# The z product of half B from bf16 parts, and the x products dealt out over the steps anew, in a gated recurrence on one core

## The chip, the cores and the metric

The kernel runs on 1 core of a Trainium2 chip. The metric is the device time of one execution in microseconds (us). Before the change it is 1654.64 us, the median of 3 runs (1654.48 to 1655.43).

## The reference

A gated recurrent layer over T = 512 time steps with batch 8, 512 inputs and 512 state units, and a residual sum at the end:

```python
def step(h, x_t):
    fused = sigmoid(concatenate([x_t, h], -1) @ w_W + w_b)
    hidden_state, output_state = split(fused, 2, -1)         # r and z
    memory_state = x_t @ wx_W + wx_b + hidden_state * (h @ wh_W + wh_b)
    h_new = output_state * h + (1.0 - output_state) * tanh(memory_state)
    return h_new, h_new
out = x + scan(step, h0, x)          # all float32; x is (8, 512, 512)
```

Below, r and z are the two gates, "h" in a bank's content is `h @ wh_W`, and x products are `x_t` times its three weight matrices, which do not depend on the state.

## The kernel before

**Layout.** State units lie on partitions. The 512 units are four chunks k = 0 to 3 of 128 inputs; half A of the state is chunks 0 and 1, half B chunks 2 and 3. Each step's matmul has a state chunk as the stationary operand (128 x 32: four steps of 8 batch columns, three of them zero) and weights as the moving one. For each k there are four products j, one on each 32-column tile of TensorE, so the outputs stand on partitions 32j to 32j+31. An f32 matmul appears in the profile as two MATMULs with a LDWEIGHTS each.

**A step on TensorE** (loop over i, from line 565; order by `ORDER`, line 26): "A0 B0 A1 A2 A3 B1 B2 B3 C0 C1 C2 C3", a bank's letter and the state chunk k. Bank A (192 columns) holds h, z and r of half A, bank B (128) r and h of half B, and C (64) z of half B. C lies in the PSUM tile `cs` (64 columns for each parity of the group of four steps). In the profile `hTA` and `hTB` are the two halves of the state, `wa` and `wb` the weights, `wb` those of B and C.

Behind C come the x products of a later pair of groups (`x_step`, line 528). A group is four steps (GS), and one x product serves a group, so that two groups are worked on over eight steps; u is the step's place in these eight and o their number. `SLOTS` names seven slots of 384 columns of products of block sums (seven products instead of eight), and `SHARE` (line 48) gives the columns for each u. The products accumulate in `xps` and `eps`; ScalarE and VectorE combine them (lines 697 to 742) into the SBUF tiles `even` and `odd`, one for each group of the pair.

**x into the banks.** `spread` (line 448) copies the group's x part from `even` or `odd` to a bank on ScalarE, once in four steps; the C copy is at u = 1, 3 (last pair) and 7. `turn_x` transposes the part that goes into the memory state (`md1`).

**A step on VectorE and ScalarE.** VectorE transposes 128x64 pieces of the banks (`turn_r`, `turn_h`, `turn_z`; tiles `tr`, `md1`, `tz`), ScalarE applies the sigmoid to `tr` (into `md0`) and `tz` (into `hd0`, with scale -1). `memory(hf, q)` is a scan on VectorE that makes the memory state `m` of chunk q of a half, and a tanh on ScalarE into the state tile (`hTA<-m`, `hTB<-m`); `update(hf, q)` is the scan that writes the new state (`hTA<-hd0A,hTA`). The order on VectorE is that of lines 655 to 677: half A's transposes and scans; r and h of half B; update(0,0); z of half B; update(0,1), which also waits for r of half B's sigmoid; memory(1,0), memory(1,1), update(1,0), update(1,1). Behind it two ScalarE copies (`hTA<-hTA`, `hTB<-hTB`) put the new state into a second slot. GpSimd adds x to the new state for the output (`ot`, lines 750 to 771), and SyncE stores four steps at a time.

**Order.** All instructions are collected by `Flow`, and each engine works through its own in the order of the program. `plan` adds semaphore waits: a reader for the last writer, a writer for readers, and for PSUM any engine for the last access of every other engine in that tile and partition quarter.

**State tiles.** `hT` are eight tiles for each half; a tile holds 32 columns (four steps) in three slots.

Of the kernel before, what the change touches and what calls it, by code (L numbers as in the profile page):

```python
# [8 lines left out]
F32 = mybir.dt.float32  # L9
# [5 lines left out]
P = 128  # L15
NQ = 4
# [70 lines left out]
class Flow:  # L87
# [44 lines left out]
    def plan(self):  # L132
# [9 lines left out]
        for i, item in enumerate(self.items):  # L142
# [70 lines left out]
            snap[me] = order[i]  # L213
            done.append(snap)

    def emit(self, tc):

        self.plan()
        sems = {e: tc.alloc_semaphore(f"flow_{e}") for e in self.ENGINES}
        lanes = [tc.alloc_semaphore(f"flow_dma{n}") for n in range(self.LANES)]  # L220
        count = {}
        with tc.tile_critical():
            for item in self.items:
                engine = getattr(self.nc, item.engine)
                for other in sorted(item.waits, key=lambda o: o.index):
                    engine.wait_ge(other.sem, other.value)
                inst = getattr(self, item.op, getattr(engine, item.op, None))(*item.args, **item.kw)  # L227
# [11 lines left out]
def tile_cond_rnn_residual(  # L239
# [132 lines left out]
    for n, t_ in enumerate(hd0[0] + hd0[1] + md0[0] + md0[1] + hT[0] + hT[1]):  # L372
        (nc.vector if n < DVE_FILL else nc.gpsimd).memset(t_, 0.0)
    for t_ in hd0[0] + hd0[1]:
        nc.gpsimd.memset(t_[:, :, :, 1], -1.0)
    idle = const.tile([P, IDLE], F32, name="idle")
# [9 lines left out]
    def state(hf, i, slot=2):  # L386
# [5 lines left out]
    wide = [{n: psum.tile([P, 512], F32, name=f"{n}{q}") for n in "AB"} for q in range(2)]  # L392
    banks = [
        {"A": wide[q]["A"][:, : BANKS["A"]],
         "B": wide[q]["B"][:, : BANKS["B"]],
         "C": cs[:, HU * q : HU * q + HU]}
        for q in range(2)
    ]
    xps = [psum.tile([P, 512], F32, name=f"xp{q}") for q in range(2)]
    piece = psum.tile([P, 512], F32, name="eps")  # L400
    eps = piece[HI, :W]

    def mm(out_, lhsT, rhs, start=False):
        nc.tensor.matmul(
# [122 lines left out]

    def x_step(o, u):

        at = sum((SHARE * 2)[5 : u if u > 4 else u + 8]) - SHARE[5] // 3  # L530
        o += 2 if u > 4 else 1
        end = at + SHARE[u]
        while at < end:
            n, c0 = divmod(at, W)
            c1 = min(W, c0 + end - at)
            for pair_, (name, k) in enumerate(SLOTS[n % 7]):
                product(o + n // 7 - (n % 7 == 0 and pair_ == 0), name, k, c0, c1)
            at += c1 - c0
# [14 lines left out]
            for t_ in (even, odd):  # L553
                nc.gpsimd.tensor_copy(t_, bias)
    keep(0)
    spread(0, "ABC")
    for hf in range(2):
        turn_x(0, hf)
    keep(1)
# [5 lines left out]
    for i in range(T):  # L565
# [8 lines left out]
        for n in (ORDER if i else FIRST).split():  # L574
            if n == "x":
                take(first[3], 1)
                continue
            bank, k = n[0], int(n[1])
            hs = hT[k // 2][i % NH][:, :, k % 2, 2]
# [9 lines left out]
        def scan(c_, out_, d0, d1):  # L589
# [8 lines left out]
        pa = ps["A"]  # L598
        raw = {
            "h": (pa[:, :HU], ps["B"][:, HU:]),  # L600
            "z": (pa[:, HU : 2 * HU], ps["C"]),
            "r": (pa[:, 2 * HU :], ps["B"][:, :HU]),
        }

# [57 lines left out]
        turn_r(1)  # L662
        turn_h(1)
        update(0, 0)
        turn_z(1)
        nc.after(update(0, 1), r_done[1])
        if i == T - 1:
            nc.gpsimd.tensor_tensor(
                ot[:, t, :2, :].rearrange("p c n -> p n c"),
# [1 line left out]
                state(0, T),  # L671
                ALU.add,
            )
        memory(1, 0)
        memory(1, 1)
        update(1, 0)
        update(1, 1)
        for hf in range(2):
            act(state(hf, i + 1, 0), state(hf, i + 1), AF.Copy)
        if i < 3:  # L680
            inst = load_x(i + 1)
            if i == 0:
                nc.after(inst, r_done[1])
# [6 lines left out]
        if o == LAST:  # L690
            if u == 2:
                spread(2 * o + 1, "AB")
                turn_x(2 * o + 1, 0)
                turn_x(2 * o + 1, 1)
            elif u == 3:
                spread(2 * o + 1, "C")
        elif u == 0:
            if o == 0:
                spread(1, "A")
            if sums:  # L700
                nc.scalar.copy(reg(BE), reg(AL))
                nc.scalar.copy(both[LO], reg(DE))
                x_sum(o + 1, 3)
            turn_x(2 * o + 1, 0)
            turn_x(2 * o + 1, 1)
        elif u == 1:
            if sums:
                nc.scalar.copy(more[HI], eps)
            spread(2 * o + 1, "BC" if o == 0 else "AC")
        elif u == 2:  # L710
            if sums:
                nc.vector.tensor_tensor(reg(GA), reg(BE), more[HI], ALU.add)
                nc.scalar.copy(even[LO, XC], reg(AL))
            if o:
                spread(2 * o + 1, "B")
        elif u == 3:
            if sums:
                nc.vector.tensor_tensor(odd[HI, XC], reg(GA), both[LO], ALU.add)
                nc.scalar.copy(both[HI], reg(DE))
            if two:  # L720
                x_sum(o + 2, 2)
        elif u == 4:
            if o == 0:
                keep(3)
            if two:
                nc.scalar.copy(reg(AL), bias[LO, XC])
                x_sum(o + 2, 0)
        elif u == 5:
            if sums:
                nc.vector.tensor_tensor(even[HI, XC], reg(BE), both[HI], ALU.add)  # L730
            if two:
                nc.scalar.copy(reg(DE), step_bias[HI])
        elif u == 6 and nxt:
            spread(2 * o + 2, "AB")
            turn_x(2 * o + 2, 0)
        elif u == 7 and nxt:
            if o:
                nc.scalar.copy(odd[LO, XC], reg(GA))
            spread(2 * o + 2, "C")
            turn_x(2 * o + 2, 1)  # L740
            if two:
                x_sum(o + 2, 1)
# [107 lines left out]
```

## Time and profile before

| | |
|---|---|
| median of 3 runs | 1654.64 us (1654.48 to 1655.43) |
| profiled execution | 1657.46 us; span of its instructions 1655.7 us |
| TensorE granted clock, mean | 0.999 |
| TensorE matmul busy | 1645.6 us (99%) |
| VectorE, ScalarE, GpSimd busy | 1153.9 (70%), 1193.8 (72%), 301.9 (18%) us |
| instructions | 125580 |

A row of the groups view names line, engine, operation, output and inputs with their shape, the count, then busy us, mean ns of one, and idle time before with what ended it. All operations have line 227 because `Flow` issues them. A row of a timeline has start in us, duration, engine, operation, output and inputs and the count of neighbours taken together; in brackets stands the wait before it and what ended that.

### The profile page before, as it was taken

How to read it: one execution, taken by the hardware profiler on the slowest of the kernel's cores; microseconds unless marked ns; L12 is line 12 of the kernel's file. 1: busy time of each engine (PE TensorE's matmuls, PEld its weight loads, DVE VectorE, ACT ScalarE, POOL GpSimd, SP SyncE). 2: the span in 40 equal slices, each digit the busy share in tenths (PEclk: the TensorE clock that was granted, in tenths of full speed). 3: DMA queues.
4: the chain of work that ended last, by engine and by line, in shares of the span. 5: the costliest groups of instructions: out<-in, count | busy, mean ns of one | idle time of the engine just before them, and what ended most of it. 6: DMA issues, size and time to landing. Idle time of an engine off the chain costs nothing.

```text
span 1655.7 us, 125580 instructions
## 1 busy us (share of the span) xinstructions
PE 1645.6 (99%) x54298; PEld 1500.2 (91%) x54298; DVE 1153.9 (70%) x9194; ACT 1193.8 (72%) x5998; POOL 301.9 (18%) x1279
## 2 busy tenths in 40 slices
PE   9999999999999999999999999999999999999998
PEld 5999999999999999999999999999999999999987
DVE  6776676676766766767667767677676766766765
ACT  3777777777777777777777777777777777777775
POOL 1211111111111111111111111111111111111111
PEclk9999999999999999999999999999999999999999
DMA  4000000000000000000000000000000000000000
GB/s 182 11 18 14 15 15 16 16 14 15 16 15 15 14 16 16 14 14 15 16 15 14 14 17 14 15 14 17 14 14 15 17 14 14 15 17 10 10 10 10
DMA packets 37284, 31.14 MB, mean 19 GB/s; under 512 B 4084, under 2 KB 35060, under 8 KB 36600
## 3 DMA queue, kind: packets, MB, share of 16 engines
q1 hardware_dynamic: 36576, 22.89, 4.5%
q8 instruction: 424, 6.95, 1.7%
q14 instruction: 132, 1.08, 0.2%
q10 hardware_dynamic: 152, 0.22, 0.1%
HBM read 14.70 MB, written 8.39 MB: 14 GB/s over the span
## 4 chain that ended last, share of the span: by engine, by line
PE 99%; DVE 1%; issue 0%; ACT 0%; DVEq 0%; SPq 0%
PE A L227 40%; PE B L227 26%; PE xp L227 18%; PE cs L227 13%; PE eps L227 1%; DVE tr L227 0%; DVE m L227 0%; DVE tz L227 0%; DVE md1B L227 0%; DVE md1A L227 0%; DVE hTA L227 0%; DVE hTB L227 0%; ACT hTB L227 0%; DVE zeros L227 0%; DVE rows L227 0%
## 5 line engine op out<-in xcount | busy, mean ns | idle before, releaser
L227 PE MATMUL A<-wa,hTA 128*32 128x192 f32 x8192 | 559.5, 326 | 2.4 <-DVE hTA L227 2.2
L227 PE MATMUL B<-wb,hTA 128*32 128x128 f32 x8192 | 454.8, 273 | 0.0
L227 PE MATMUL A<-wa,hTB 128*32 128x192 f32 x8192 | 448.6, 326 | 0.0
L227 PEld LDWEIGHTS A<-wa,hTA 128*32 128x32 f32 x8192 | 292.5, 122 | 124.6 <-DVE hTA L227 101.7
L227 DVE STREAM_TRANSPOSE tr<-A 128x64 f32<-128x64 f32 x512 | 128.0, 250 | 367.6 <-PE A L227 367.6
L227 POOL TENSOR_TENSOR ot<-xin,hTB 128x16 f32<-128x16 f32 x495 | 123.8, 250 | 1290.4 <-DVE hTB L227 1290.4
L227 PEld LDWEIGHTS B<-wb,hTA 128*32 128x32 f32 x8192 | 352.6, 122 | 2.8 <-issue 0.3
L227 PE MATMUL B<-wb,hTB 128*32 128x128 f32 x8192 | 339.6, 273 | 0.0
L227 PEld LDWEIGHTS A<-wa,hTB 128*32 128x32 f32 x8192 | 330.4, 122 | 9.1 <-DVE hTB L227 0.2
L227 ACT ACTIVATE md0A<-tr 128x16 f32<-128x16 f32 x512 | 112.4, 219 | 238.5 <-DVE tr L227 238.4
L227 PE MATMUL xp<-tw,sx 128*32 128x384 f32 (+2 forms) x1464 | 269.7, 433 | 0.0
L227 PEld LDWEIGHTS B<-wb,hTB 128*32 128x32 f32 x8192 | 262.3, 122 | 0.2 <-issue 0.2
L227 PE MATMUL cs<-wb,hTB 128*32 128x64 f32 x8192 | 230.3, 219 | 0.4 <-issue 0.3
L227 PE MATMUL cs<-wb,hTA 128*32 128x64 f32 x8192 | 230.2, 219 | 0.0
L227 DVE TENSOR_TENSOR_SCAN hTB<-hd0B,hTB 128x24 f32<-128x24 f32 x1024 | 158.0, 196 | 99.8 <-ACT hTB L227 99.8
L227 PE MATMUL xp<-wx,xin 128*32 128x384 f32 (+4 forms) x1348 | 219.1, 413 | 0.0
L227 PEld LDWEIGHTS cs<-wb,hTA 128*32 128x32 f32 x8192 | 207.5, 122 | 0.0
L227 DVE TENSOR_TENSOR_SCAN hTA<-hd0A,hTA 128x24 f32<-128x24 f32 x1024 | 190.9, 186 | 0.0
L227 ACT ACTIVATE hd0B<-tz 128x16 f32<-128x16 f32 x512 | 115.6, 226 | 94.5 <-DVE tz L227 94.5
L227 PEld LDWEIGHTS cs<-wb,hTB 128*32 128x32 f32 x8192 | 180.2, 122 | 0.7 <-issue 0.7
L227 ACT ACTIVATE hTB<-hTB 128x16 f32<-128x16 f32 x512 | 120.3, 235 | 79.1 <-DVE hTB L227 72.8
L227 ACT ACTIVATE hTA<-m 128x8 f32<-128x8 f32 x1024 | 160.8, 206 | 0.6 <-DVE m L227 0.3
(101 smaller groups left out, 2680.6 us busy)
## 6 DMA issues: line engine op xcount, KB each, us to landing
out_dram<-ot SPq DMA_DIRECT2D x128, 64.0 KB, 1.6
xin<-in_x_dram SPq DMA_DIRECT2D x112, 64.0 KB, 2.4
wx<-in_wx_dram SPq DMA_DIRECT2D x4, 768.0 KB, 7.0
wa<-in_wa_dram SPq DMA_DIRECT2D x4, 384.0 KB, 9.8
wb<-in_wb_dram SPq DMA_DIRECT2D x1, 1152.0 KB, 13.7
xin<-in_x_dram SPq DMA_DIRECT2D x3, 256.0 KB, 3.7
wb<-in_wb_dram SPq DMA_DIRECT2D x1, 384.0 KB, 14.1
head<-in_xh_dram ACTq DMA_DIRECT2D x1, 208.0 KB, 4.7
```

The costliest lines, as they stand in the source:

```text
L227: inst = getattr(self, item.op, getattr(engine, item.op, None))(*item.args, **item.kw)
```

## The change

z of half B (bank C) is computed, from step `PLAIN` = 3 on, by bf16 matmuls. The new state is split by truncation: `split` holds h, h minus its upper 16 bits, and that again minus its upper 16 bits, and the upper halves of these three (8 batch columns each, 24 columns) are the stationary operand, read from the f32 words with a step of two elements. The moving operands are the upper halves of `wb`, `w2` and `w3`, made in the same way once in step 0. `kept` issues a MATMUL on the weights that are already loaded, so that a k and j take one LDWEIGHTS and three MATMULs of 64 columns. Four GpSimd subtractions a step make `split`, two per half.

The output then lies on 24 rows of each 32: the three parts of the state times 8. VectorE's transpose `tzB` is followed by a new `tensor_reduce` over the four blocks of 8 columns, into `tzs`, from which ScalarE takes the sigmoid. Each step has a C cell of its own in `cs` (eight in turn), filled by `spread_c`: an ACTIVATE per step with a scale `mask` per partition, which leaves x in that step's 8 rows. There are two in eight steps before (COPY) and eight after, at u = 0, 1 (two), 2 (two), 6 and 7 (two).

On VectorE, memory(1,0) and the reduce now stand between z's transpose and update(0,1). `SHARE` is dealt out as below; its sum stays 2688. State tiles of the two halves become one tile of 64 columns, of which the upper 32 stay zero. Of the first memsets, six of eight state tiles are on VectorE and two on GpSimd.

```diff
-DVE_FILL = 23
+DVE_FILL = 14
-BANKS = {"A": 192, "B": 128, "C": 64}
+BANKS = {"A": 192, "B": 128}
+PLAIN = 3
-SHARE = [384, 384, 384, 384, 288, 288, 288, 288]
+SHARE = [306, 384, 384, 384, 308, 306, 308, 308]
+EARLY = 76
...
+    def kept(self, out, lhsT, rhs):
+        t = self.nc.tensor
+        return t.add_instruction(
+            mybir.InstMatmult(
...
+                tile_size=(128, 32),
+                tile_position=(0, out.offset // 512 // 32 * 32),
+                ldweights=False,
...
-    hT = [[pair(n, f"hT{n}{i}", 32, 3) for i in range(NH)] for n in "AB"]
+    hs = [const.tile([P, NQ, 64, 3], F32, name=f"hT{i}") for i in range(NH)]
+    hT = [[t_[:, 2 * n : 2 * n + 2, :32].rearrange("p c n s -> p n c s") for t_ in hs] for n in range(2)]
+    split = [const.tile([P, NQ, 3, B], F32, name=f"split{i}") for i in range(2)]
+    w2 = const.tile([P, NQ, NQ, HU], F32, name="w2")
+    w3 = const.tile([P, NQ, NQ, HU], F32, name="w3")
+    mask = const.tile([P, GS, 32], F32, name="mask")
...
+    def parts(out_, i, k, j):
+        lhsT = high(split[i % 2])[:, k].rearrange("p u b -> p (u b)")[:, 1::2]
+        for n, t_ in enumerate((wb[:, k, j, :HU], w2[:, k, j], w3[:, k, j])):
+            (nc.tensor.kept if n else mm)(out_, lhsT, high(t_)[:, 1::2])
...
+    def cell(i):
+        return cs[:, HU * (i % NH) : HU * (i % NH) + HU]
+
+    def spread_c(g, steps_):
+        for s in steps_:
+            nc.scalar.activation(
+                cell(GS * g + s), source(g)[:, XP["C"]], AF.Copy, scale=mask[:, s, :1]
+            )
...
-        at = sum((SHARE * 2)[5 : u if u > 4 else u + 8]) - SHARE[5] // 3
+        at = sum((SHARE * 2)[5 : u if u > 4 else u + 8]) - EARLY
...
-                mm(ps[bank][32 * j : 32 * j + 32, :], hs, wh(bank, k, j))
+                if bank == "C" and i >= PLAIN:
+                    parts(cell(i)[32 * j : 32 * j + 24], i, k, j)
+                else:
+                    to = cell(i) if bank == "C" else ps[bank]
+                    mm(to[32 * j : 32 * j + 32, :], lhsT, wh(bank, k, j))
...
         def turn_z(hf):
-            tz, _ = turned("z", hf)
+            if hf:
+                t_, tz = tzb, tz_sum
+                nc.vector.tensor_reduce(
+                    tz, t_.rearrange("p c (u b) -> p c b u", u=4), mybir.AxisListType.X, ALU.add
+                )
+            else:
+                tz, _ = turned("z", hf)
...
         update(0, 0)
+        tzb = work.tile([P, 2, 32], F32, tag="tzB", name=f"tzB_{i}")
+        tz_sum = work.tile([P, 2, B], F32, tag="tzs", name=f"tzs_{i}")
+        nc.vector.transpose(tzb.rearrange("p c n -> p (c n)"), raw["z"][1])
+        memory(1, 0)
         turn_z(1)
-        nc.after(update(0, 1), r_done[1])
+        update(0, 1)
...
-        memory(1, 0)
         memory(1, 1)
         update(1, 0)
         update(1, 1)
         for hf in range(2):
             act(state(hf, i + 1, 0), state(hf, i + 1), AF.Copy)
+            if PLAIN <= i + 1 < T:
+                ks, s1 = slice(2 * hf, 2 * hf + 2), B * ((i + 1) % GS)
+                t_, new = split[(i + 1) % 2][:, ks], hs[(i + 1) % NH][:, ks]
+                nc.gpsimd.tensor_tensor(
+                    t_[:, :, :2].rearrange("p k u b -> p k b u"),
+                    new[:, :, s1 : s1 + B, 2].unsqueeze(3).broadcast_to([P, 2, B, 2]),
+                    high(new).rearrange("p k (u n) s -> p k n u s", u=2)[:, :, s1 : s1 + B, :, 5],
+                    ALU.subtract,
+                )
+                nc.gpsimd.tensor_tensor(t_[:, :, 2], t_[:, :, 0], high(t_)[:, :, 0, 1::2], ALU.subtract)
+        if i == 0:
+            for to, t_ in ((w2, wb[:, :, :, :HU]), (w3, w2)):
+                nc.gpsimd.tensor_tensor(to, t_, high(t_)[:, :, :, 1::2], ALU.subtract)
...
         elif u == 0:
...
+                spread_c(2 * o, (2,))
...
         elif u == 1:
...
-            spread(2 * o + 1, "BC" if o == 0 else "AC")
+            spread(2 * o + 1, "B" if o == 0 else "A")
+            if o:
+                spread_c(2 * o, (3,))
+            spread_c(2 * o + 1, (1,) if o else (0, 1))
         elif u == 2:
...
+            spread_c(2 * o + 1, (2, 3))
...
             spread(2 * o + 2, "AB")
+            spread_c(2 * o + 2, (0,))
...
-            spread(2 * o + 2, "C")
+            spread_c(2 * o + 2, (1,))
+            if o + 1 < LAST:
+                spread_c(2 * o + 3, (0,))
```

More of the change, by code (lines that the diff above doesn't have):

```diff
@@ L214, in plan @@
             done.append(snap)
+    def kept(self, out, lhsT, rhs):
+        t = self.nc.tensor
+        return t.add_instruction(
+            mybir.InstMatmult(
+                name=self.nc.get_next_instruction_name(),
+                ins=[t.lower_ap(rhs), t.lower_ap(lhsT)],
+                outs=[t.lower_ap(out)],
+                start_tensor_calc=False,
+                stop_tensor_calc=False,
+                tile_size=(128, 32),
+                tile_position=(0, out.offset // 512 // 32 * 32),
+                bass_skip_group_check=True,
+                ldweights=False,
+                engine=mybir.EngineType.PE,
+            )
+        )
     def emit(self, tc):
@@ L371, in tile_cond_rnn_residual @@
     nc.scalar.activation(const.tile([P, 1], F32, name="table"), zeros[:, :1], AF.Sigmoid)
-    for n, t_ in enumerate(hd0[0] + hd0[1] + md0[0] + md0[1] + hT[0] + hT[1]):
+    for n, t_ in enumerate(hd0[0] + hd0[1] + md0[0] + md0[1] + hs):
         (nc.vector if n < DVE_FILL else nc.gpsimd).memset(t_, 0.0)
+    steps = const.tile([P, GS, 32], F32, name="steps")
+    nc.vector.memset(steps, 0.0)
+    for n in range(GS):
+        nc.vector.memset(steps[:, n, B * n : B * n + B], 1.0)
+    nc.vector.transpose(mask.rearrange("p s n -> p (s n)"), steps.rearrange("p s n -> p (s n)"))
     for t_ in hd0[0] + hd0[1]:
@@ L555, in tile_cond_rnn_residual @@
     keep(0)
-    spread(0, "ABC")
+    spread(0, "AB")
+    spread_c(0, range(GS))
     for hf in range(2):
@@ L600, in tile_cond_rnn_residual @@
             "h": (pa[:, :HU], ps["B"][:, HU:]),
-            "z": (pa[:, HU : 2 * HU], ps["C"]),
+            "z": (pa[:, HU : 2 * HU], cell(i)),
             "r": (pa[:, 2 * HU :], ps["B"][:, :HU]),
@@ L695, in tile_cond_rnn_residual @@
             elif u == 3:
-                spread(2 * o + 1, "C")
+                spread_c(2 * o + 1, (0, 1))
+            elif u == 4:
+                spread_c(2 * o + 1, (2, 3))
+            elif u < 2:
+                spread_c(2 * o, (2 + u,))
         elif u == 0:
@@ L699, in tile_cond_rnn_residual @@
                 spread(1, "A")
+            else:
+                spread_c(2 * o, (2,))
             if sums:
@@ L715, in tile_cond_rnn_residual @@
                 spread(2 * o + 1, "B")
+            spread_c(2 * o + 1, (2, 3))
         elif u == 3:
```

9 lines of the change are left out of this document (6 added, 3 removed).

## The prediction

> **What bounds the kernel now.** First the page: the chain of waits lies on TensorE almost to the end.
>
> ```profile
> span 1655.7 us, 125580 instructions
> ...
> PE 99%; DVE 1%; issue 0%; ACT 0%; DVEq 0%; SPq 0%
> ```
>
> That share is an average over two kinds of step, so next the timeline of ScalarE over five steps. The sigmoid `md0A<-tr` comes once a step, a fixed time after the A products end, so its starts measure the steps.
>
> ```profile
> 839.74 0.24 ACT L227 ACTIVATE hTB<-hTB 128x16 f32<-128x16 f32 x1 [0.15 <-DVE hTB L227]
> 839.99 0.45 ACT L227 COPY xp<-xp 64x384 f32<-64x384 f32 x1
> 840.47 0.48 ACT L227 COPY both<-xp 64x384 f32<-64x384 f32 x1
> 841.14 0.22 ACT L227 ACTIVATE md0A<-tr 128x16 f32<-128x16 f32 x1 [0.19 <-DVE tr L227]
> ...
> 843.25 0.47 ACT L227 COPY more<-eps 64x384 f32<-64x384 f32 x1
> 843.74 0.32 ACT L227 COPY A<-odd 128x192 f32<-128x192 f32 x1
> 844.00 0.21 ACT L227 COPY cs<-odd 128x64 f32<-128x64 f32 x1
> 844.40 0.22 ACT L227 ACTIVATE md0A<-tr 128x16 f32<-128x16 f32 x1 [0.20 <-DVE tr L227]
> ...
> 846.52 0.47 ACT L227 COPY even<-xp 64x384 f32<-64x384 f32 x1
> 846.89 0.26 ACT L227 COPY B<-odd 128x128 f32<-128x128 f32 x1
> 847.67 0.22 ACT L227 ACTIVATE md0A<-tr 128x16 f32<-128x16 f32 x1 [0.51 <-DVE tr L227]
> ...
> 850.93 0.22 ACT L227 ACTIVATE md0A<-tr 128x16 f32<-128x16 f32 x1 [0.65 <-DVE tr L227]
> ...
> 854.04 0.22 ACT L227 ACTIVATE md0A<-tr 128x16 f32<-128x16 f32 x1 [0.63 <-DVE tr L227]
> ```
>
> The distances are 3.26, 3.27, 3.26 and 3.11 us. Steps with 384 columns of x (heavy) take 3.265, those with 288 (light) 3.11: the 96 columns cost 0.16, 1.6 ns each. Four of each in eight give a mean of 3.187. Third, TensorE inside a light step:
>
> ```profile
> 802.42 0.40 PE L227 MATMUL cs<-wb,hTA 128*32 128x64 f32 x15
> ...
> 802.87 0.25 PE L227 MATMUL xp<-tw,xin 128*32 128x96 f32 x1
> ...
> 803.36 0.55 PE L227 MATMUL A<-wa,hTA 128*32 128x192 f32 x8
> ```
>
> C takes 0.45 (802.42 to 802.87), x 0.49, so the A and B products take 3.11 - 0.94 = 2.17. Last, steps near the end, where almost nothing but the recurrence runs:
>
> ```profile
> 1643.86 0.41 PE L227 MATMUL cs<-wb,hTA 128*32 128x64 f32 x16
> ...
> 1644.73 0.55 PE L227 MATMUL A<-wa,hTA 128*32 128x192 f32 x8 [0.24 <-DVE hTA L227]
> ...
> 1645.64 0.83 PE L227 MATMUL A<-wa,hTB 128*32 128x192 f32 x16
> ```
>
> ```profile
> 1643.46 0.25 DVE L227 STREAM_TRANSPOSE tr<-A 128x64 f32<-128x64 f32 x1 [0.94 <-PE A L227]
> ...
> 1644.59 0.22 DVE L227 STREAM_TRANSPOSE tz<-cs 128x64 f32<-128x64 f32 x1
> 1644.74 0.17 DVE L227 TENSOR_TENSOR_SCAN hTA<-hd0A,hTA 128x24 f32<-128x24 f32 x1
> ...
> 1645.27 0.31 DVE L227 TENSOR_TENSOR_SCAN hTB<-hd0B,hTB 128x24 f32<-128x24 f32 x2 [0.19 <-ACT hTB L227]
> ...
> 1646.54 0.25 DVE L227 STREAM_TRANSPOSE tr<-A 128x64 f32<-128x64 f32 x1 [0.94 <-PE A L227]
> ```
>
> ```profile
> 1643.74 0.22 ACT L227 ACTIVATE md0A<-tr 128x16 f32<-128x16 f32 x1 [0.97 <-DVE tr L227]
> ...
> 1644.85 0.22 ACT L227 ACTIVATE hd0B<-tz 128x16 f32<-128x16 f32 x1 [0.18 <-DVE tz L227]
> 1645.03 0.32 ACT L227 ACTIVATE hTB<-m 128x8 f32<-128x8 f32 x2
> ...
> 1645.62 0.23 ACT L227 ACTIVATE hTB<-hTB 128x16 f32<-128x16 f32 x1 [0.15 <-DVE hTB L227]
> ```
>
> TensorE waits here 0.24 us for `hTA`, and the step is 3.08 (1643.46 to 1646.54). That is the recurrence of half A: A products, transposes, sigmoid, scan, tanh, update. It contains no C and no x, so the change can't shorten it. A light step now lies only 0.03 above it.
>
> **The change part by part.** *C products.* Sixteen f32 products (two passes each) become 48 bf16 passes of the same 64 columns, 12 instead of 8 on each of the four column tiles. The f32 pass takes 0.45/8 = 0.056 us.
>
> ```profile
> L227 PE MATMUL xp<-wx,xin 128*32 128x384 f32 x732 | 149.9, 486 | 0.0
> ...
> L227 PE MATMUL cs<-wb,hTA 128*32 128x64 f32 x8192 | 230.2, 219 | 0.0
> ...
> L227 ACT COPY A<-odd 128x192 f32<-128x192 f32 x63 | 20.4, 324 | 0.7
> ...
> L227 ACT COPY cs<-odd 128x64 f32<-128x64 f32 x63 | 13.2, 209 | 0.0
> ...
> L227 PE MATMUL xp<-zeros 128*128 128x512 f32 x4 | 3.7, 1074 | 0.0
> ...
> L227 PE MATMUL cs<-none 128*128 128x512 bf16 x1 | 0.6, 610 | 2.3 <-DVE none L227 2.3
> ```
>
> From 486 and 219 ns a column costs 0.834 ns in f32, with 166 ns fixed. At the start one shape ran in both types: (1074 - 166)/(610 - 166) = 2.0, so bf16 takes half per column. Estimate: 64 x 0.417 + 3 = 0.029 a pass, 12 passes 0.35, 0.10 saved. Bounds: 0.35, and 12 x 0.056 = 0.67 if bf16 read at a stride of two elements goes no faster than f32. I take 0.35, since the row is bf16.
>
> *x dealt out anew.* Work is unchanged (2688 columns in eight steps). With the C saving a heavy step has 3.165 of TensorE, a light one 3.11 - 0.10 + 18 x 0.0016 = 3.035. The mean of TensorE's work is 3.084, about the recurrence's 3.08: from here on the recurrence counts in the five light steps.
>
> *Half B's order on VectorE.* The transpose of C stays (1644.59); in the place of the update at 1644.74 goes the memory scan, then the new reduce, and `update(0,1)` and the second scan come behind. The reduce needs the transpose landed: 1644.59 + 0.22 + 0.03 = 1644.84. No reduce is in the trace; nearest are the 0.17 scan and the 0.22 transpose of 64 elements. The sigmoid then starts at 1645.04 to 1645.09 (hand-over 0.03, seen between `tz` and `hd0B`), ends 0.22 later, and `update(1,0)` starts at 1645.29 to 1645.34 instead of 1645.27: 0.02 to 0.07 late. Its weight load followed it by 0.26 and the matmuls at 1645.64 by 0.11 more, of which a load needs some 0.04, so 0.07 late is still in time: 0 to 0.04 a step with the bound a little beyond, I take 0.01, a light step of 3.09. `update(0,1)` moves by 0.25 to about 1644.98; A1 is due one A chunk (2 x 192 x 0.834 = 0.32) before 1645.64, at 1645.32, so its 0.26 to the weight load and 0.04 more just fit. The state copy `hTB<-hTB` (1645.62) goes 0.05 later with the updates.
>
> *GpSimd.* Four subtractions a step, of the size of the two adds it has; half A's can start at some 1645.2 and take about 0.25 each, half B's 0.3 later, all done by 1646.3, and C is due at 1644.73 + 2.17 = 1646.90. But they run beside half B's scans, which they did not before. Nearest rows, from the first steps:
>
> ```profile
> 30.52 0.59 DVE L227 TENSOR_TENSOR_SCAN m<-md0A,md1A 128x16 f32<-128x16 f32 x2
> ...
> 31.32 0.24 DVE L227 TENSOR_TENSOR_SCAN hTA<-hd0A,hTA 128x24 f32<-128x24 f32 x1
> ```
>
> ```profile
> 29.97 1.02 POOL L227 TENSOR_TENSOR stepbias<-bias,stepbias 64x384 f32<-64x384 f32 x1 [3.26 <-ACT stepbias L227]
> ...
> 31.26 0.24 POOL L227 TENSOR_TENSOR ot<-head,hTA 128x16 f32<-128x16 f32 x1
> ```
>
> Scans beside the long subtraction took 0.59 instead of some 0.28, until it ended; the update beside a small add 0.24 instead of 0.20. So a split costs an update 0.04, at most its own 0.25. I take 0 on the path, because the split must still be reading when `update(1,0)` starts; the bounds go to the rivals. The Trainium skill, "SBUF — State Buffer", section "Who interferes with whom", says that a VectorE instruction with two SBUF inputs contends with a GpSimd instruction that reads SBUF; the scan of 0.59 agrees.
>
> *w2 and w3*, two GpSimd operations of 1024 elements, by the 1.02 for 384 some 2.7 us each, run once beside the scans and weight sums of the first step: 0 to 5.4 us, I take 3. The other fills lie ahead of the first A, which waits for x.
>
> *x of z on ScalarE.* Two copies of 128x64 per eight steps become eight ACTIVATEs with a scale read from SBUF. They stand behind the `hTB` copy, ahead of the next `md0A`, and C now waits for the last of them (one PSUM bank). Between the clean `hTB` copy (1645.62) and the next `md0A` (1646.54 + 0.28) lie 1.20 us, after the change 1.16 by the 0.05 above; C is due 0.12 later (1643.86 against 1643.74), 1.28. Where TensorE made the step before heavy, both are 0.075 later (3.165 - 3.09). An instruction that changes partition half starts 0.01 after the end of the one ahead (839.74 to 839.99, 843.25 to 843.74), another 0.10 before that end (846.52 to 846.89), or 0.06 behind a copy into PSUM (843.74 to 844.00). For the new one I take the same copy's 0.209, and 0.324 (the 128x192 copy) as the other end. The step after u = 0: 0.13 + 0.21 + 0.01 + 0.48 + 0.38 = 1.21 for 1.16, covered by the heavy step. After u = 1: 0.25 + 0.49 + 0.26 + 0.15 + 0.21 + 0.09 for the hand-over = 1.45 for 1.355: C stalls 0.10, step 3.265. After u = 2: 0.25 + 0.37 + 0.19 + 0.15 + 0.21 + 0.09 = 1.26, in time. After u = 6 and 7 there is less.
>
> *Sum.* (5 x 3.09 + 3.165 + 3.265 + 3.165)/8 = 3.131, 0.056 less than 3.187. Over the 488 steps between the first 8 and the last 16: -27.3. The other 24 steps +0.2, the start +3: -24. The profiled execution took 1657.46 (span 1655.7), so 1633.4; the median shown is 2.8 below it: 1631.
>
> **The rivals.** *Whole gain:* ScalarE and VectorE are in time everywhere, light steps 3.08, heavy ones 3.165, mean 3.112: 1621. For it: only the step after u = 1 misses, and by 0.10. Against it: VectorE gets one more instruction in series.
>
> *Late C:* the new ACTIVATE takes 0.324. Then the step after u = 0 is 3.25, after u = 1 C stalls 0.40 (3.56), after u = 2 0.095 (3.26); mean 3.19, time 1659, and the gain is gone from about 0.31 on. The row for the same shape, 0.209, speaks against it. The Trainium skill, "ScalarE: Activation LUTs", section "What ACT_TABLE_LOAD costs", adds some 93 ns for a scale read per partition; that would make it 0.30 and the time about 1653. No scaled copy is in the trace.
>
> *Held update, the other side:* the split of half A catches `update(1,0)` in every step. It can start 0.03 or more after `update(0,1)` ends, from 1644.98 + 0.17 + 0.03 = 1645.18 on, and the update is due at 1645.29 to 1645.34. Held by 0.04 to 0.25, the update passes its 0.07 of cover; at 0.08 beyond it a light step is 3.17, the heavy ones 3.22, 3.40 and 3.20, mean 3.209: 1669. It decides from a light step of 3.14 on. For it speak the rows at 30.52 and 31.32, against it how small the splits are.
>
> *C no shorter:* if tiles hold each other up so that C keeps 0.45, light steps are 3.135, heavy 3.265 and one 3.365: 1662; at 0.67, 1764. The f32 tiles run side by side, which speaks against it.
>
> **How the numbers follow.** Forecast 0.45 (1623 to 1645), whole gain 0.20, late C 0.14, held update 0.12, C no shorter 0.05, something unnamed 0.04, half on each side. The range 1614 to 1668 takes in the whole gain, late C and nearly the held update. A measurement here tells 0.2% (3.3 us) from no change. Faster: 0.45 + 0.20 + 0.02 and a part of late C, 0.69; same, from late C alone, 0.07; slower 0.24.
>
> **What would show it.** C from its first matmul to the first of x: 0.35 (0.45 or more: C no shorter). Light steps 3.08 to 3.10 between `tr` and `tr`, with TensorE waiting on `hTA`. `hTB<-hd0B` waiting for ScalarE's `hd0B`, not the tanh. The step after u = 1 longest, its C weights waiting on ScalarE's copy into `cs`. Wrong it would be most by scans of half B longer than 0.21 beside `split`, by ACTIVATEs into `cs` over 0.30, or by A's `hTB` weights late.

## The result and the profile after

The changed kernel takes 1731.62 us (median of 4 runs, 1730.51 to 1732.49), the kernel before 1654.87 beside it: a ratio of 1.0463 (95% interval 1.0445 to 1.0481). It is slower by 77 us, and 101 us above the 1631 forecast. Its page:

```profile
span 1728.7 us, 130138 instructions
...
PE 54%; ACT 25%; DVE 18%; issue 3%; DMA 0%; DVEq 0%; ACTq 0%; SPq 0%
```

Of the chain of waits 99% lay on TensorE before, and now 54%: a quarter is ScalarE's and 18% VectorE's. TensorE is no longer the bound in most steps.

Step lengths are taken in what follows from the start of one `tr<-A` to the next, as medians over the rounds of eight steps. After: the three steps behind the work of u = 0, 1 and 2 take 3.41, 3.67 and 3.49 us, the others 3.16 to 3.20. Before they were 3.265 (four) and 3.105 to 3.11 (four). No step became shorter than the light step of before.

ScalarE in the steps behind u = 0, 1 and 2 (columns as before):

```profile
903.98 0.23 ACT L249 ACTIVATE hT<-hT 128x16 f32<-128x16 f32 x1
904.11 0.30 ACT L249 ACTIVATE cs<-even,mask 128x64 f32<-128x64 f32 x1
904.44 0.45 ACT L249 COPY xp<-xp 64x384 f32<-64x384 f32 x1
904.91 0.47 ACT L249 COPY both<-xp 64x384 f32<-64x384 f32 x1
905.36 0.22 ACT L249 ACTIVATE md0A<-tr 128x16 f32<-128x16 f32 x1
...
907.46 0.23 ACT L249 ACTIVATE hT<-hT 128x16 f32<-128x16 f32 x1 [0.15 <-DVE hT L249]
907.70 0.47 ACT L249 COPY more<-eps 64x384 f32<-64x384 f32 x1
908.19 0.32 ACT L249 COPY A<-odd 128x192 f32<-128x192 f32 x1
908.44 0.31 ACT L249 ACTIVATE cs<-even,mask 128x64 f32<-128x64 f32 x1
908.69 0.30 ACT L249 ACTIVATE cs<-odd,mask 128x64 f32<-128x64 f32 x1
909.02 0.22 ACT L249 ACTIVATE md0A<-tr 128x16 f32<-128x16 f32 x1
...
911.11 0.23 ACT L249 ACTIVATE hT<-hT 128x16 f32<-128x16 f32 x1 [0.15 <-DVE hT L249]
911.36 0.47 ACT L249 COPY even<-xp 64x384 f32<-64x384 f32 x1
911.73 0.26 ACT L249 COPY B<-odd 128x128 f32<-128x128 f32 x1
911.93 0.55 ACT L249 ACTIVATE cs<-odd,mask 128x64 f32<-128x64 f32 x2
912.42 0.20 ACT L249 ACTIVATE md0A<-tr 128x16 f32<-128x16 f32 x1
```

The three `md0A` rows have no bracket: ScalarE did not wait for VectorE's transpose, it came late from its own queue. TensorE beside the second of them:

```profile
909.14 0.22 PE L249 MATMUL cs<-wb,split 128*24 128x64 bf16 x4 [0.28 <-ACT cs L249]
...
909.49 0.50 PE L249 MATMUL xp<-wx,xin 128*32 128x384 f32 x2
```

C waits for ScalarE's copy into `cs`, as the rival "late C" had it. In the medians, `md0A` is 0.24 late behind u = 0 and C is in time; behind u = 1 both are 0.49 late, behind u = 2 C 0.32 and `md0A` 0.23. C itself is as forecast, 909.14 to 909.49, 0.35 us. The prices, from the groups (line, engine, operation, count, busy us, mean ns, idle before):

```profile
L249 DVE TENSOR_REDUCE tzs<-tzB 128x16 f32<-128x64 f32 x512 | 138.2, 270 | 0.4
...
L249 ACT ACTIVATE cs<-even,mask 128x64 f32<-128x64 f32 x252 | 77.6, 309 | 0.0
...
L249 ACT ACTIVATE cs<-odd,mask 128x64 f32<-128x64 f32 x252 | 72.3, 303 | 0.0
```

A light step on VectorE, with ScalarE's sigmoid, tanh and state copy and TensorE's weight loads of A beside it:

```profile
915.40 0.25 DVE L249 STREAM_TRANSPOSE tr<-A 128x64 f32<-128x64 f32 x1 [0.20 <-PE A L249]
...
916.53 0.23 DVE L249 STREAM_TRANSPOSE tzB<-cs 128x64 f32<-128x64 f32 x1
916.68 0.15 DVE L249 TENSOR_TENSOR_SCAN m<-md0B,md1B 128x16 f32<-128x16 f32 x1
916.79 0.27 DVE L249 TENSOR_REDUCE tzs<-tzB 128x16 f32<-128x64 f32 x1
...
917.35 0.39 DVE L249 TENSOR_TENSOR_SCAN hT<-hd0B,hT 128x24 f32<-128x24 f32 x2
...
918.57 0.25 DVE L249 STREAM_TRANSPOSE tr<-A 128x64 f32<-128x64 f32 x1 [0.80 <-PE A L249]
```

```profile
917.10 0.23 ACT L249 ACTIVATE hd0B<-tzs 128x16 f32<-128x16 f32 x1
917.29 0.21 ACT L249 ACTIVATE hT<-m 128x8 f32<-128x8 f32 x1
...
917.78 0.23 ACT L249 ACTIVATE hT<-hT 128x16 f32<-128x16 f32 x1 [0.16 <-DVE hT L249]
...
918.85 0.22 ACT L249 ACTIVATE md0A<-tr 128x16 f32<-128x16 f32 x1 [0.46 <-DVE tr L249]
```

```profile
917.23 0.19 PEld L249 LDWEIGHTS A<-wa,hT 128*32 128x32 f32 x8
917.63 0.49 PEld L249 LDWEIGHTS A<-wa,hT 128*32 128x32 f32 x13 [0.21 <-DVE hT L249]
```

From the transpose the reduce starts 0.26 later, the sigmoid 0.57, the update of half B 0.82 (before 0.26 to the sigmoid and 0.68 to the update, 1644.59, 1644.85, 1645.27). TensorE then waits 0.21 in the middle of A, for half B's state. The step is 3.17 although C, x and half A have time: the recurrence now runs through half B.

### The profile page after: what moved, and what is told of

Read it like the earlier page. It is cut to its first block, busy times and chain, and to the rows that moved or that the text cites. A ratio compares the mean times of both kernels' runs of the same rounds, so it can differ in the third digit from the quotient of the medians.

```text
span 1728.7 us, 130138 instructions
## 1 busy us (share of the span) xinstructions
PE 1684.9 (97%) x62930; PEld 1320.3 (76%) x46642; DVE 1329.8 (77%) x9703; ACT 1330.4 (77%) x6382; POOL 771.2 (45%) x3318
## 3 DMA queue, kind: packets, MB, share of 16 engines
q8 instruction: 429, 7.03, 1.7%
## 4 chain that ended last, share of the span: by engine, by line
PE 54%; ACT 25%; DVE 18%; issue 3%; DMA 0%; DVEq 0%; ACTq 0%; SPq 0%
PE A L249 24%; PE B L249 13%; PE xp L249 9%; DVE hT L249 6%; ACT hT L249 6%; ACT cs L249 5%; DVE m L249 5%; PE cs L223 4%; PE cs L249 3%; ACT hd0B L249 3%; DVE tr L249 3%; ACT md0A L249 2%; DVE md1B L249 2%; ACT even L249 2%; DVE tzB L249 2%
## 5 line engine op out<-in xcount | busy, mean ns | idle before, releaser
L249 PE MATMUL A<-wa,hT 128*32 128x192 f32 x16384 | 900.1, 333 | 6.8 <-DVE hT L249 6.7
L249 PEld LDWEIGHTS A<-wa,hT 128*32 128x32 f32 x16384 | 488.6, 125 | 260.0 <-DVE hT L249 193.2
L249 PE MATMUL B<-wb,hT 128*32 128x128 f32 x16384 | 647.0, 273 | 0.5 <-issue 0.5
L249 POOL TENSOR_TENSOR split<-hT 128x32 f32<-128x32 f32 x1018 | 264.2, 259 | 849.0 <-DVE m L249 837.6
L249 PEld LDWEIGHTS B<-wb,hT 128*32 128x32 f32 x16384 | 528.6, 122 | 35.4 <-DMA wb<-in_wb_dram 1.0
L249 ACT ACTIVATE hT<-m 128x8 f32<-128x8 f32 x2048 | 379.9, 210 | 172.4 <-DVE m L249 144.8
L249 ACT ACTIVATE hT<-hT 128x16 f32<-128x16 f32 x1024 | 230.7, 225 | 79.4 <-DVE hT L249 76.5
L249 PE MATMUL cs<-wb,split 128*24 128x64 bf16 x8144 | 255.6, 193 | 26.1 <-ACT cs L249 16.9
L223 PE MATMUL cs<-w,split 128*24 128x64 bf16 x16288 | 272.2, 192 | 2.2 <-issue 1.9
L249 PE MATMUL xp<-tw,sx 128*32 128x384 f32 (+4 forms) x1708 | 263.1, 395 | 0.0
```

What stands on the lines that cost most here:

```text
L223: return t.add_instruction(mybir.InstMatmult(name=self.nc.get_next_instruction_name(), ins=[t.lower_ap(rhs), t.lower_ap(lhsT)], outs=[t.lo ...
```

## The experiments

Two theories stood at the start. S: the eight dearer spreads make ScalarE late, `md0A` and C with it. R: the reduce, in series ahead of half B's sigmoid, makes each step late. A third, F, on TensorE's instruction stream, came out of the first four runs. All ratios are against the kernel before, run beside them (1654.9 us beside the changed kernel, 1656.7 to 1657.9 beside the others), with 95% intervals.

| kernel | us | ratio (interval) |
|---|---|---|
| changed kernel | 1731.6 | 1.0463 (1.0445 to 1.0481) |
| e1_copy: spreads without mask | 1705.8 | 1.0284 (1.0266 to 1.0303) |
| e2_vec: spreads on VectorE | 1685.1 | 1.0166 (1.0145 to 1.0186) |
| e3_nosum: no reduce | 1685.8 | 1.0166 (1.0151 to 1.0181) |
| e4_vec_nosum: both | 1655.5 | 0.9997 (0.9982 to 1.0013) |
| e5_full: e2, placed better, w2 and w3 in pieces | 1664.7 | 1.0047 (1.0032 to 1.0062) |
| e6_nosum: e5 without the reduce | 1640.6 | 0.9906 (0.9883 to 0.9929) |
| e7_mixed: e6, C between B's blocks | 1675.7 | 1.0118 (1.0101 to 1.0135) |
| e8_half: bf16 C in four steps of eight | 1656.7 | 0.9995 (0.9986 to 1.0005) |
| e9_half_vec: e8, one spread to VectorE | 1647.0 | 0.9933 (0.9922 to 0.9945) |

**e1_copy**

```diff
-            nc.scalar.activation(
-                cell(GS * g + s), source(g)[:, XP["C"]], AF.Copy, scale=mask[:, s, :1]
-            )
+            nc.scalar.copy(cell(GS * g + s), source(g)[:, XP["C"]])
```

> The changed kernel, but ScalarE spreads the x part into C's cells with a plain copy and no mask (left out: the mask, so that C also takes the x of the other three steps of its group). It takes .10 us from each of the eight instructions of a round (309 ns to 209), and moves nothing. Theory S (the spreads make ScalarE late, md0A and C with it): of the delays of md0A, .24, .49 and .23 us after the work of steps 0, 1 and 2 of a round, .10 to .20 each go; the excess of 1.08 us a round falls to about .5; 61 rounds: 1732 - 35 = about 1697 (1690 to 1705). Theory R (the reduce in series ahead of half B's sigmoid makes every step late, and what ScalarE has left to do only follows that): the spreads' price is not what counts, 1720 or more.

1705.8, 26 us off against 35 expected. The three steps went from 3.41, 3.67, 3.49 to 3.32, 3.48, 3.29: 0.09, 0.19, 0.20 less, the 0.1 per spread. Of the missing 9 us, 5.5 are steps irregularly above the median of their kind (14.5 us against 9 in the changed kernel), which theory F below is about. So the mask's 0.1 us is real, but more than half of the excess (0.61 of 1.13 us a round) is not the mask: with plain copies, six more than before, ScalarE is still late.

**e2_vec**

```diff
-            nc.scalar.activation(
-                cell(GS * g + s), source(g)[:, XP["C"]], AF.Copy, scale=mask[:, s, :1]
+            nc.vector.tensor_scalar(
+                cell(GS * g + s), source(g)[:, XP["C"]], mask[:, s, :1], None, ALU.mult
...
-            spread_c(2 * o + 1, (1,) if o else (0, 1))
+            spread_c(2 * o + 1, (1, 2, 3) if o else (0, 1, 2, 3))
...
-            spread_c(2 * o + 1, (2, 3))
```

> The changed kernel with the masked spread into C's cells on VectorE instead of ScalarE, and the odd group's last two cells spread after step 1 of a round instead of step 2. The reduce and GpSimd's splits stay. S: the steps that take 3.41, 3.67 and 3.49 us fall to the 3.165 to 3.20 of the others, mean 3.325 to 3.17 over 472 steps: 1732 - 73 = about 1658 (1652 to 1670). R alone: ScalarE is late because half B is late, which stays: over 1690.

1685.1, not 1658. Seven steps of eight did what S said: 3.16 to 3.195. The eighth, the step of u = 7, went from 3.16 to 3.50, which costs 61 x 0.33 = 20 us, and that was the edit's own doing; its row in the waits (waiter, released by, us in total, times, longest):

```profile
DVE cs L249 <- ACT odd L249: 36.9, 61, 0.6
```

VectorE works in order and waited once a round for ScalarE's copy of the x part into `odd`, with the next step's transposes queued behind.

**e3_nosum**

```diff
-                t_, tz = tzb, tz_sum
-                nc.vector.tensor_reduce(
-                    tz, t_.rearrange("p c (u b) -> p c b u", u=4), mybir.AxisListType.X, ALU.add
-                )
+                tz = tzb[:, :, :B]
```

> The changed kernel without the reduce: the sigmoid of half B's z reads the first of the three parts' columns straight from the transpose (left out: the sum of the parts). The spreads stay on ScalarE with their mask. S and R together: every step loses the .085 us by which half A's last update came late (3.165 to 3.08, 41 us), and half B's last copy comes about .1 us earlier in the step, which takes some .3 us a round from the excess of 1.08 (18 us): 1732 - 59 = about 1673 (1663 to 1685); the steps after the work of steps 0 to 2 stay .1 to .4 longer than the others. S alone: only the 18 us, 1714. R alone: both go, the excess as well, about 1625 to 1640.

1685.8. The medians did what S and R together said: light steps 3.08, the three late ones 3.19, 3.49 and 3.275. The medians alone save 66 us, where 59 were expected for both. But steps irregularly above the median of their kind made up 30 us (9 in the changed kernel, 2 before), which takes 21 back, and that is why 1673 was missed. Neither S nor R has a place for them.

**e4_vec_nosum** has the edits of e2_vec and e3_nosum.

> Both edits at once: the spread into C's cells on VectorE and no reduce (left out: the sum of the parts). GpSimd's splits, the w2 and w3 parts, the twelve short bf16 passes and the new dealing of the x products stay. S and R together: every step at the 3.08 of the recurrence of half A, 1732 - 472 x .24 = about 1619 (1612 to 1630), some 9 us of it still lost at the start and the end against the kernel before. A rival K (what costs is something else that the change brought: GpSimd's splits beside VectorE's scans, or changes between f32 and bf16 on TensorE): over 1650.

1655.5, and so on the side of K: something else does cost. Light steps take 3.07 to 3.09, as S and R say. Steps with 384 columns take 3.18, 0.015 above the 3.165 that the forecast had for TensorE's own work there; the expectation of 3.08 in every step left that out (18 us); the step of u = 7 is 3.29 (e2's misplaced spread, 13 us), and irregular steps add 18 us, 9 more than in the changed kernel. It is not what K named: GpSimd's splits, and changes between f32 and bf16 on TensorE, stand in every one of the 3.08 steps, so they hold nothing up there.

*Theory F.* Where the irregular gaps lie in TensorE's stream can be counted in the traces. The page gives the block in which instructions are fetched (queue, kind: packets, MB, share):

```profile
q8 instruction: 429, 7.03, 1.8%
```

7.03 MB in 429 packets is 16.4 KB each, and TensorE's 109572 matmuls and loads over 429 are 255; from these two counts the queue is taken to be TensorE's. Counted together with TensorE's few hundred semaphore instructions, the gaps fall into place: in the thirteen traces 152 instructions of C start 0.30 us or more behind another of C, and all 152 stand at the same place modulo 256 (in e6_nosum the first of the two stalls shown below follows instruction 14273, 55 x 256 + 193). The other crossings are counted on from there. About 120 of them fall in C's passes; there the step and the one after it are longer by 0.16 us together in e4_vec_nosum (14 us of its excess of 18, each step counted once), and by 0.10 in the changed kernel (nearly all of its 9). A crossing inside A or B costs at most 0.05 in these two, and one inside f32 C, in the kernel before, 0.02.

The packets of this queue say more. At no crossing of any trace, from the second on, does TensorE go on sooner than 1.17 us after the last packet ended. At the 152 long gaps it goes on 1.17 to 1.68 us after that (median 1.39), at the 1210 crossings in C without a gap of 0.10 at a median of 1.93. So a long gap looks like a wait for a block whose packet came late; no run moves a packet by itself. Why the stalls fall in C is argued: its 64 instructions now take 0.35 us, the fastest stretch of the stream.

**e5_full**: e2_vec with the odd group's first cell spread after u = 0, and w2 and w3 in pieces.

```diff
-PLAIN = 3
+PLAIN = 8
...
-        if i == 0:
-            for to, t_ in ((w2, wb[:, :, :, :HU]), (w3, w2)):
-                nc.gpsimd.tensor_tensor(to, t_, high(t_)[:, :, :, 1::2], ALU.subtract)
+        if i < PLAIN:
+            n, k = divmod(i, NQ)
+            to, t_ = ((w2, wb[:, :, :, :HU]), (w3, w2))[n]
+            inst = nc.gpsimd.tensor_tensor(to[:, k], t_[:, k], high(t_)[:, k, :, 1::2], ALU.subtract).ins
+            nc.after(inst, late)
...
             turn_x(2 * o + 1, 1)
+            if o:
+                spread_c(2 * o + 1, (0,))
...
-            if o + 1 < LAST:
-                spread_c(2 * o + 3, (0,))
```

(`late` is the last scan of the step.)

> The changed kernel complete, with its spreads on VectorE and two more edits: the odd group's first cell is spread after step 0 of a round (in e2_vec it stood after step 7, where VectorE waited .6 us for ScalarE's copy of the odd x part and that step took 3.50 us), and w2 and w3 are made in eight pieces in the first eight steps, each behind the last scan of its step (C stays f32 until then). Theory S+R: no step is left that waits for a spread, every step stands at the 3.16 to 3.18 that the reduce sets; 1685 - 61 x .33 - 4 for the start = about 1661 (1655 to 1668). If the start is lost otherwise than by GpSimd's two long operations beside VectorE's scans, its first four steps still take 19 us together instead of 14.6.

1664.7. All eight steps stand at 3.16 to 3.195, and the first four take 15.2 us together (19.6 in the changed kernel, 14.6 before). Here is why the changed kernel lost them, VectorE and GpSimd in its first step:

```profile
21.30 1.60 DVE L249 TENSOR_TENSOR_SCAN hT<-hd0A,hT 128x24 f32<-128x24 f32 x1
...
22.98 1.88 DVE L249 TENSOR_TENSOR_SCAN m<-md0B,md1B 128x16 f32<-128x16 f32 x1
```

```profile
20.48 2.37 POOL L249 TENSOR_TENSOR w<-wb 128x1024 f32<-128x1024 f32 x1 [8.99 <-DMA wb<-in_wb_dram]
22.92 1.89 POOL L249 TENSOR_TENSOR w<-w 128x1024 f32<-128x1024 f32 x1
```

Each scan lasted until the GpSimd operation beside it ended (20.48 + 2.37 = 22.85, 22.92 + 1.89 = 24.81), which agrees with the Trainium skill, "SBUF — State Buffer", "Who interferes with whom": a VectorE instruction with two SBUF inputs contends with a GpSimd instruction that reads SBUF.

**e6_nosum** is e5_full with e3's edit.

> The same without the reduce (left out: the sum of the parts). S+R: steps with 384 x columns 3.18, all others 3.08; 1655 - 61 x .21 - 4 = about 1638 (1632 to 1645). The distance to e5_full is then what the reduce costs by itself, 23 us; R as first put (.085 in each of 488 steps) gives 41, less what the steps that TensorE bounds at 3.18 hide, four of eight: 21 to 25.

1640.6, so that the reduce by itself costs 24 us, inside the 21 to 25 expected (by the two intervals, give or take some 5 us). The medians of the steps alone give 61 x 0.43 = 26; irregular steps work against that, 22 us here against 9 in e5_full. A light step on VectorE:

```profile
921.67 0.25 DVE L249 STREAM_TRANSPOSE tr<-A 128x64 f32<-128x64 f32 x1 [0.16 <-PE A L249]
...
922.80 0.22 DVE L249 STREAM_TRANSPOSE tzB<-cs 128x64 f32<-128x64 f32 x1
...
923.49 0.31 DVE L249 TENSOR_TENSOR_SCAN hT<-hd0B,hT 128x24 f32<-128x24 f32 x2 [0.21 <-ACT hd0B L249]
...
924.75 0.25 DVE L249 STREAM_TRANSPOSE tr<-A 128x64 f32<-128x64 f32 x1 [0.93 <-PE A L249]
```

The update follows the transpose by 0.69 instead of 0.82, and the step is 3.08. The chain of waits is TensorE's again:

```profile
PE 97%; DVE 2%; issue 1%; ACT 0%; DVEq 0%; SPq 0%
```

**e7_mixed**

```diff
-ORDER = "A0 B0 A1 A2 A3 B1 B2 B3 C0 C1 C2 C3"
+ORDER = "A0 B0 A1 A2 A3 B1 C0 B2 C1 B3 C2 C3"
```

> e6_nosum with TensorE's order of a step changed: C's passes of each block stand between B's blocks instead of behind them all (A0 B0 A1 A2 A3 B1 C0 B2 C1 B3 C2 C3). Theory F: the irregular long steps (18 us in e4_vec_nosum over the median of each kind of step, against 2 before) are TensorE's instruction stream at the seam of two fetched blocks of 256 instructions: 64 instructions in .35 us leave it no lead, and a seam that falls among them stalls it by .3 to .6 us. With half as many short instructions in a row the excess falls to about 10 or less: 1630 (1624 to 1635). A rival (the stalls come from transfers or from GpSimd): the excess stays, 1638. If B's later end holds up half B's transposes, each step is up to .1 longer and the run above 1650.

1675.7: the bad case. With C's passes ahead of B's end, `tr<-B` starts 0.86 after `tr<-A` instead of 0.73, half B is late again and every step is 3.20 to 3.21. The excess over the medians did fall, from 22 to 10.5 us, as F says, but steps that wait for half B anyway may also hide stalls, so this run does not show F by itself.

**e11_same and e10_shift** do. e11_same is e6_nosum again; e10_shift adds, ahead of the first x products,

```diff
+    for _ in range(64):
+        mm(xps[1][:, :1], none, none[:, :1])
```

> e6_nosum once more, unchanged: how many of the 72 steps (of steps 17 to 487) that stood over .10 us above the median of their kind are long again. F: the seams of TensorE's instruction blocks lie at the same instructions, so about half or more of them (35 and up; kernels that share TensorE's stream, the changed one and e3_nosum, share 27 of the changed one's 39); if the stalls fall by chance, 72 x 72 / 471 = 11.

> e6_nosum with 64 pairs of weight load and one-column bf16 product of zeros put ahead of the first x products on TensorE (128 instructions, half a block of 256; they add zero, and lengthen the start by some 3 to 5 us). Every seam then falls 128 instructions earlier in the work. F: the long steps are other ones, no more than chance in common with e6_nosum's 72 (11, against the unchanged repeat's half), while their sum (22 us) stays within some 6 us. A rival, that the long steps come from transfers or from GpSimd at fixed steps: the same steps as in the unchanged repeat are long again.

Long steps: 72 in e6_nosum, 61 in its repeat, 22 in common (chance: 72 x 61 / 471 = 9). That is well above chance but below the 35 expected: a crossing stalls only at times. In e10_shift there are 71, of which 8 in common with e6_nosum (chance 11) and 6 with the repeat (9), while their excess stays (24.7 us against 22.4 and 20.6). The steps, and with them the transfers and GpSimd's work, are the same in all three; only the crossings moved, and with its added pairs counted e10_shift's gaps stand at the same place modulo 256 as the others. The same stall in e6_nosum and in its repeat, C's passes on TensorE in one step:

```profile
225.42 0.25 PE L223 MATMUL cs<-w,split 128*24 128x64 bf16 x5
225.92 0.19 PE L223 MATMUL cs<-w,split 128*24 128x64 bf16 x1 [0.25 <-issue]
```

```profile
227.00 0.23 PE L223 MATMUL cs<-w,split 128*24 128x64 bf16 x5
227.49 0.19 PE L223 MATMUL cs<-w,split 128*24 128x64 bf16 x1 [0.25 <-issue]
```

Both times TensorE stops behind the same instruction, number 14233 of its matmuls and loads, and starts no other for 0.45 us; "issue" says that nothing the profile shows held it. The two single runs took 1644.6 (e11_same) and 1651.9 us (e10_shift); a few us of the second are its 64 added pairs.

**e8_half**: bf16 C only in the steps of the even group, from the second round on; the odd group as before the change, shares of before.

```diff
+    def short(i):
+        return PLAIN <= i < T and i % NH < GS
+
     def cell(i):
-        return cs[:, HU * (i % NH) : HU * (i % NH) + HU]
+        n = i % NH if short(i) else GS + i // GS % 2
+        return cs[:, HU * n : HU * n + HU]
...
-SHARE = [306, 384, 384, 384, 308, 306, 308, 308]
+SHARE = [384, 384, 384, 384, 288, 288, 288, 288]
...
-                if bank == "C" and i >= PLAIN:
+                if bank == "C" and short(i):
...
-            if hf:
+            if hf and short(i):
```

(Splits, reduce and the order on VectorE likewise hang on `short`; the even cells are spread two each after u = 6 and 7.)

> A complete kernel in which only the four steps of a round with 384 x columns have C's product in bf16 parts (spreads of their cells on VectorE in the steps before, where VectorE has time, w2 and w3 as in e5_full, reduce and VectorE's order of the changed kernel), while the other four keep f32 C, one cell for the group, one plain spread, no split, no reduce, the order of before, and the shares of before, 384 and 288. S+R+F: four steps of 3.18 and four of 3.105, mean 3.143 against 3.190 before: 1657 - 488 x .047 + about 5 for the seams = 1639 (1630 to 1648), faster than both kernels. If a step that follows one of the other kind pays for its neighbour's late half B, 1650 or more.

1656.7, no gain. Seven steps came as expected (3.18 three times, 3.105 to 3.11 four times); the step behind u = 1 took 3.335, and irregular steps cost 10 us where 5 were put. ScalarE ahead of that step's `md0A`:

```profile
866.89 0.48 ACT L249 COPY more<-eps 64x384 f32<-64x384 f32 x1
867.38 0.32 ACT L249 COPY A<-odd 128x192 f32<-128x192 f32 x1
867.64 0.21 ACT L249 COPY cs<-odd 128x64 f32<-128x64 f32 x1
867.88 0.22 ACT L249 ACTIVATE md0A<-tr 128x16 f32<-128x16 f32 x1
```

This is the very queue that the kernel before has in time. Half B's later end (the step of u = 1 still has the reduce) is enough to make it late, with one plain copy.

**e9_half_vec**

```diff
-            nc.scalar.copy(cell(GS * g), source(g)[:, XP["C"]])
+            copy = nc.vector.tensor_copy if 0 < g // 2 < LAST else nc.scalar.copy
+            copy(cell(GS * g), source(g)[:, XP["C"]])
```

> e8_half with one edit: the plain spread of the odd group's C cell after step 1 of a round goes from ScalarE to VectorE. In e8_half that spread stood on ScalarE until .41 us into the next step, put md0A off by .15 us, and made that step 3.335 us where its kind takes 3.18. S: this step falls to 3.18, 61 x .15 = 9 us: 1656.7 - 9 = about 1648 (1644 to 1652), against before .9945. If the step is long for another reason it stays at 3.33 and the run at 1657.

1647.0, ratio 0.9933 (0.9922 to 0.9945): faster than both kernels, as expected. On VectorE, in the first of the two fences, the copy stands in idle time; ScalarE is then through with the odd group's A copy just as `md0A` is due:

```profile
837.29 0.21 DVE L249 COPY cs<-odd 128x64 f32<-128x64 f32 x1
...
838.21 0.25 DVE L249 STREAM_TRANSPOSE tr<-A 128x64 f32<-128x64 f32 x1 [0.65 <-PE A L249]
```

```profile
838.15 0.33 ACT L249 COPY A<-odd 128x192 f32<-128x192 f32 x1
838.50 0.22 ACT L249 ACTIVATE md0A<-tr 128x16 f32<-128x16 f32 x1
```

The step is 3.18; the round is 4 x 3.18 and 4 x 3.11.

## Why the prediction was wrong

The forecast's sum for a round of eight steps was 25.05 us (8 x 3.131), with the irregular steps of the kernel before, 0.03, on top. The changed kernel's medians add up to 26.45, and irregular steps to 0.15 more, 26.60. Where the 1.52 came from:

| term of a round | predicted | measured | us in 61 rounds |
|---|---|---|---|
| steps ahead of any ScalarE delay | 5 x 3.09 + 3 x 3.165 = 24.95 | 8 x 3.165 = 25.32 | +23 |
| delays behind ScalarE's queue | 0.10 | 1.13 | +63 |
| irregular steps (block crossings) | 0.03, as before | 0.15 | +7 |

With 2 us more at the start (5 for the 3 put on w2 and w3), 2 in the last 16 steps, and 4 because the forecast took the median to lie 2.8 below the profiled execution, where the changed kernel's lies 1.1 above its own, that is the 101 us.

*What bounds the kernel, and C: right.* The recurrence of half A at 3.08 and 0.35 us for twelve bf16 passes stood; e6_nosum has 3.08 in light steps, and 3.18 with 384 columns, where 3.165 was put. "C no shorter" is out.

*Half B's order: the step that failed first.* The reduce was put at 0.17 to 0.22, from a scan and a transpose; it takes 0.270, and the hand-over to the sigmoid 0.04 where 0.03 was put. The sigmoid comes 0.57 behind the transpose instead of 0.45 to 0.50, the update 0.82 to 0.84 instead of 0.70 to 0.75. The cover of 0.07 was about right, so that 0.075 of the mis-sized 0.1 went through to the step: 3.165, not 3.09. e5_full against e6_nosum shows it alone, 24 us. The state copy then comes about 0.22 late, not 0.05: 0.14 with the update, and most of the rest because half B's second update waits for a tanh that ScalarE now runs behind the late sigmoid (917.29).

*x of z on ScalarE: the step that cost most.* Three terms were off at once. The spread takes 0.303 to 0.309 instead of 0.209: the Trainium skill's 93 ns for a per-partition scale ("ScalarE: Activation LUTs", "What ACT_TABLE_LOAD costs") agrees with this trace's 94 to 100, and the row of the nearest shape was the wrong one to take. The window from the state copy to `md0A`, put at 1.16, is 1.07 (917.78 to 918.85), because half B is late. And the 0.075 allowed behind a heavy step is not there, since half B sets those steps as well. For the step behind u = 1: 907.46 to 909.02 is 1.56, 0.49 over the 1.07, and the step is 3.67, 0.51 over 3.165. The steps behind u = 0 and u = 2, put "covered" and "in time", are 0.24 and 0.33 over. S and R are not independent: the spreads moved away save 47 us (e2_vec, about 67 without its misplaced one), the reduce taken out 46 (e3_nosum), both 76 (e4_vec_nosum, 89 without the misplaced one).

*Late C as a rival* had the mechanism, the place and even the price (0.30), but 1653 to 1659 with it: it too went by a light step of 3.09 and the old window. *Held update* had a light step of 3.17, and its sign, a scan of half B over 0.21 beside `split`, came too; the number agreed by luck. The split does start 0.1 ahead of the update in each step, but the update takes 216 ns instead of 208, 0.01 where 0.04 to 0.25 was put, and without the reduce the light step is 3.08 with the splits in place. *GpSimd's splits at no cost* was right to that 0.01 (the second update, which does not set the step, takes 208 instead of 183). *w2 and w3*, put at 3 with an upper end of 5.4, cost 4.4 (e5_full's first four steps), by scans held up for 1.60 and 1.88 us, as the row of 0.59 had shown in small.

*The range*, up to 1668, was summed from rivals one at a time. Late spreads and a late half B feed each other, and no case had both.

*What stays open:* why the packet of an instruction block comes late at one crossing and not at the next, or not at the same one in another execution. That the crossings are where TensorE stalls is shown by the count and the shift; that the short bf16 passes leave it no lead is argued from the rates alone.

## What to carry to other kernels

When an operation is put in series on the second-longest chain, look at what follows that chain's end: here 0.1 us too much on half B's sigmoid moved a copy, the copy moved ScalarE's whole queue, and that queue had 0.2 us to spare before. Add up the queue of an in-order engine with all rivals' late starts in at once, and not each with the others at their best. A gain in one engine's work is worth having only in the steps which that engine bounds: bf16 C in the four heavy steps alone, with its by-work on the idle engine, gave 0.7%, where bf16 C everywhere lost 0.5% with the same placing (e5_full) and 4.6% as first written.

## What the hardware showed that was not expected

- TensorE's instruction stream stalls at crossings that lie 256 instructions apart when they fall in short bf16 passes: gaps of 0.3 to 0.9 us, which come 1.2 to 1.7 us behind the end of the last instruction packet. The steps at such crossings make up most of the 9 to 30 us of irregular steps in a run of 429 crossings, against 2 us with f32 passes in their place.
- A reduce of 64 to 16 elements per partition takes 0.270 us on VectorE, longer than the transpose of the same 64 elements (0.228).
- A VectorE scan beside a long GpSimd subtraction ended with it, at 1.60 and 1.88 us for some 0.2; beside subtractions of 16 and 32 elements half B's first update lost 8 ns (208 to 216).
